# Two graph layers on one core: weight loads, the logit scale, and the first and last pairs of batches rearranged

## The chip, the core and the metric

The kernel runs on one core of one Trainium2 chip. The metric is the device time of one execution in microseconds (us), the median over repeated runs. A profile is one execution recorded by the hardware profiler; its times of single instructions are used below. Five engines work in parallel: PE (matrix products; its weight loads are listed as PEld), DVE (vector), ACT (activation functions, copies with scale and bias), POOL (a second vector engine) and SP (issues transfers). [...]

## The reference, cut to what matters

There are 128 batches of 128 nodes with 512 features, and an adjacency matrix (128 x 128) for each batch. Everything is float32.

```python
# layer 0: 8 heads of 64
q, k, v = (inputs @ W + b for W, b in ((Wq, bq), (Wk, bk), (Wv, bv)))
logits = where(adj > 0, q @ k.T / sqrt(64), -1e9)
out = relu((softmax(logits) @ v) @ Wo + bo)
x = layernorm(x + out)
# layer 1
Wh = x @ W
e = leaky_relu((Wh @ a1)[:, None] + (Wh @ a2)[None, :], 0.2)
h = softmax(where(adj == 0, -1e9, e)) @ Wh
x = layernorm(x + elu(h))
```

## The kernel before

**Pairs and half-size products.** The work is done in 64 pairs of batches (pair p holds batches 2p and 2p+1, called image 0 and image 1 here). The rows of the two images and the halves of the features make a 2 x 2 matrix of blocks on the left, and each weight matrix is cut into 2 x 2 blocks on the right. The product of both is formed with seven block products in place of eight (a scheme of Strassen's kind). That needs sums of left blocks (`left_sums`, L147 to L156: `x_sums`, `o_sums`, `z_sums`, four POOL instructions a pair, on DVE for the last pair), sums of weight blocks (`weight_sums`, L131 to L136, once for each weight: `sums_qk`, `sums_v`, `sums_o`, `sums_w`; the third sum overwrites the block in slot 5 of the tile), and evictions that add partial results. `PRODUCTS` (L139) lists the seven products with their PSUM bank (A, B or C), their left block and their weight slot. Products `qk0` to `qk6` make q and k together with the tile `wqk` (Wq in slots 0 and 1, Wk in slots 5 and 2), `v0` to `v6`, `o0` to `o6` and `w0` to `w6` use `wv_b`, `wo_b` and `w_b`. The evictions are named `p1`, `p1q`, `p1l`, `p6`, `p7`, `c11`, `c12`, `c21`, `c22`. A bank can be written again only when its eviction has read it.

**The stages of a pair.** `load_blocks` and `x_transpose` (DVE) bring x in transposed; `x_sums`; qk products and evictions; `logits` (PE), `mask_logits`, `max_logits` (DVE), `exp_logits`, `norm_logits` (ACT), `weights_t` (DVE) with `weights_out` and `weights_in` (SP: to HBM and back, which finishes the transposition); `mix_values` (PE) and `mix_values_out` (ACT); o products; residual, layer norm (`stats0`, `mean0`, `rstd0`, `shift0`, `norm0`); `edge_term`, `edge_blocks`, `edge_row` (SP), `edge_sums` (ACT), `edge_leaky`, `edge_mask`, `edge_max`, `edge_exp`, `edges_t`, `edges_t_out`, `edges_t_in`; `mix_nodes` (PE) and `mix_nodes_out` (ACT, L630); w products; `elu_exp`, `elu_low`, `elu_max`, `residual1`, the second layer norm and `store`. `mix_values`, `mix_nodes` and the transposed edge weights of the last pair share one PSUM tile named `ps`.

**The two ends.** Pair 0 has no weight sums yet: `qk_plain` (L305) forms its q and k with eight plain products `qk0` to `qk3`, of Wq slot 0, Wq slot 1, Wk slot 5 and Wk slot 2, each for image 0 and image 1. `fold_a`, `fold_t` and `fold_out` (L203 to L225) work out W @ a1 and W @ a2 once: DVE, then four PE transposes each, then ACT. The last pair transposes its softmax weights and its edge weights on PE (L476, L594), and its left sums and two of its elementwise steps run on DVE (`side_engine`, L143).

**What sets the order.** The engines' queues are not filled pair by pair. Each step has a due time: `p * PERIOD + PLAN[step]`, in a planner's unit (78.77 a pair), plus a shift from `ENDS` for pairs near an end; `ENDS` is empty here. All steps of all pairs are sorted by due time (L713) and issued in that order, so each engine's queue is its share of that list. Between pairs 3 and 59 the order repeats; near the ends it is the same list with the missing pairs left out. The weight loads and the scaling of Wq by 1/8 (L198) stand before the list.

Of the kernel before, what the change touches and what calls it, by code (L numbers as in the profile page):

```python
# [17 lines left out]
PERIOD = 78.77  # L18
PLAN = dict(
    load_adj=-214.28, load_blocks=-156.46, x_transpose0=-118.96, x_transpose1=-64.06, qk0=-36.02, x_sums=-35.84,  # L20
    qk1=-32.98, qk_p1=-31.71, fill_logits0=-31.52, sums_v=-30.63, qk4=-28.65, qk_p6=-28.53, qk_p1q=-27.7,
    qk2=-26.32, qk_c11=-24.89, qk3=-22.63, v0=-21.4, qk_p7=-19.94, qk_c22=-19.93, qk5=-14.75, qk6=-13.44,
    qk_c21=-7.89, qk_c12=-7.85, sums_fold1=-6.69, v_p1=-4.73, v1=-4.54, fill_logits1=-1.85, mask=-1.24, v_p6=-0.29,
    logits=0.0, mask_logits0=2.0, max_logits0=3.74, sums_fold_t1=4.13, v3=4.41, v_p7=4.43, v2=7.45, v4=9.21,
    v_c11=9.21, mask_logits1=10.04, load_x1=10.32, v5=13.29, v_c22=14.67, exp_logits0=14.75, v_c21=15.09, v6=17.23,
    v_c12=17.58, max_logits1=22.12, sum_logits0=24.06, norm_logits0=27.41, exp_logits1=33.3, sums_qk=38.84,
    weights_t0=43.7, sum_logits1=43.78, sums_fold_out1=45.25, sums_fold0=46.53, norm_logits1=52.01,
    weights_out0=53.62, weights_t1=55.61, sums_fold_t0=63.24, weights_out1=68.01, weights_in0=70.44,
    sums_fold_out0=71.92, weights_in1=74.3, mix_values0=75.85, sums_w=78.52, mix_values_out0=80.72,
    mix_values1=81.43, mix_values_out1=85.44, load_x0=87.17, sums_o=94.72, o_sums=101.64, o0=106.22, o_p1=113.64,  # L30
    o1=113.67, o4=115.87, o_p6=116.22, o_p1l=117.15, o3=117.16, o_p7=117.32, o2=117.77, o_c11=118.24, o_c22=118.29,
    o5=120.85, o6=121.7, o_c21=121.88, o_c12=122.76, residual01=122.76, stats01=122.82, mean01=123.85,
    residual00=127.73, rstd01=128.28, shift01=128.77, stats00=130.31, norm01=131.24, mean00=131.45, rstd00=133.98,
    edge_term01=134.39, shift00=135.59, edge_term11=137.39, norm00=140.45, edge_term10=144.28, edge_blocks=146.15,
    fill_edges=152.96, edge_row=155.48, edge_term00=159.96, edge_sums=163.39, edge_leaky=169.07, edge_mask=175.0,
    edge_max=179.3, edge_exp=184.85, edges_t=185.93, edges_t_out=188.28, edges_t_in=189.77, mix_nodes1=211.95,
    mix_nodes_out1=218.25, mix_nodes0=220.51, mix_nodes_out0=222.79, z_sums=231.06, w0=248.23, edge_norm=250.39,
    w_p1=253.84, w1=254.02, w2=254.75, w_p6=256.75, w3=258.71, w_c11=259.13, w4=262.95, w_p7=264.55, w5=268.2,
    w_c22=268.29, w6=268.5, w_c21=269.01, w_c12=270.9, elu_exp1=288.36, elu_exp0=298.97, elu_low1=307.12,
    elu_max1=314.12, elu_low0=326.19, elu_max0=338.66, residual10=340.21, stats10=349.64, mean10=349.96,  # L40
    residual11=350.83, rstd10=358.93, stats11=386.25, mean11=395.88, shift10=413.33, rstd11=414.6, shift11=416.7,
    finish0=436.56, finish1=440.87, store0=451.59, store1=492.12)

ENDS = {}

BUFS = dict(
    xb=2, adj=5, xT=3, t=2, scr=1, cw=6, sx=1, pr=2, qT=2, kT=2, mask=2, e1a256=1, u2256=1, cv=2, u3256=1, prb=1,
    e1a512=1, e1b512=1, u2512=1, u3512=1, prT=2, oT=2, so=1, x=3, at=1, e1b256=1, co=6, ejr=1, e=1, atb=1, attT=1,
# [4 lines left out]
def tile_two_graph_layers(ctx: ExitStack, tc: tile.TileContext, x, adj, wq, bq, wk, bk, wv, bv, wo, bo, w, a, out,  # L53
# [36 lines left out]
    def load_blocks(p):  # L90

        XB[p] = buf([P, 2, 4, P], F32, "xb", f"xb_{p}")
        for k in range(4):
            nc.sync.dma_start(XB[p][32 * k:32 * k + 32].rearrange("s i v e -> s (i v) e"), bass.AP(
                tensor=x.tensor, offset=x.offset + 2 * p * P * D + k * P, ap=[[D, 32], [32 * D, 8], [1, P]]))

# [19 lines left out]

    def block_weight(name, width):
        return const.tile([P, 7, 2, width], F32, tag=name, name=name)

    def load_block(t, k, queue, src, rows, cols):  # L120
        for c in range(2):
            queue.dma_start(t[:, k, c, :], src[rows * HALF + c * P:rows * HALF + (c + 1) * P, cols])

    def load_block_x(t, k, queue, src, rows, cols):

        for q in range(4):
            queue.dma_start(t[32 * q:32 * q + 32, k, :, :], bass.AP(
                tensor=src.tensor, offset=src.offset + (q * P + 64 * rows) * D + cols.start,
                ap=[[D, 32], [32 * D, 2], [1, cols.stop - cols.start]]))

    def weight_sums(t, eng):  # L131
        b11, b21, b22, t1, t2, t3, t4 = (t[:, k, :, :] for k in range(7))
        eng.tensor_tensor(t1, t3, b11, op=ALU.subtract)
        eng.tensor_tensor(t2, b22, t1, op=ALU.subtract)  # L134
        eng.tensor_tensor(t3, b22, t3, op=ALU.subtract)
        eng.tensor_tensor(t4, b21, t2, op=ALU.subtract)  # L136
# [10 lines left out]
    def left_sums(tag, p, store):  # L147

        s = SUMS[tag, p] = buf([P, 4, 2, P], F32, f"s{tag}", f"s{tag}_{p}")
# [23 lines left out]
    load_block_x(wqk, 0, nc.scalar, wq, 0, everything)  # L173
    load_block_x(wqk, 1, nc.scalar, wq, 1, everything)
    load_block_x(wqk, 5, nc.sync, wk, 0, everything)
    load_block_x(wqk, 2, nc.sync, wk, 1, everything)
    load_adj(0)
    wv_b, wo_b, w_b = (block_weight(n, HALF) for n in ("wv", "wo", "w"))
    for t, src, load in ((wv_b, wv, load_block_x), (wo_b, wo, load_block), (w_b, w, load_block)):
        load(t, 0, nc.sync, src, 0, lo)  # L180
        load(t, 5, nc.sync, src, 0, hi)
        load(t, 1, nc.sync, src, 1, lo)
        load(t, 2, nc.sync, src, 1, hi)
        if t is wv_b:
            load_blocks(1)
            load_adj(1)
# [10 lines left out]
    for k in range(2):  # L197
        nc.vector.tensor_scalar_mul(wqk[:, k, :, :], wqk[:, k, :, :], qscale)  # L198
# [4 lines left out]
    def fold_a(i):  # L203
# [3 lines left out]
        for c in range(NC):  # L207
            for f in range(2):
                scr = buf([P, HALF], F32, "scr", f"wa_scr{i}_{c}_{f}")
                blk = ((0, 5), (1, 2))[c // 2][f]  # L210
                nc.vector.scalar_tensor_tensor(scr, w_b[:, blk, c % 2, :], 1.0, a_bc[:, f * HALF:(f + 1) * HALF],
                                               op0=ALU.mult, op1=ALU.mult, accum_out=wa[:, f, c:c + 1])
# [10 lines left out]
    def fold_out(i):  # L223
        wa_bc[i] = const.tile([P, D], F32, tag=f"wa_bc{i}", name=f"wa_bc{i}")
        nc.scalar.copy(wa_bc[i], ST.pop(("wa", i)).rearrange("p c k -> p (c k)"))  # L225

# [15 lines left out]
    def rows_product(blk, weight, left, j):  # L242
# [4 lines left out]
        for c in range(2):  # L247
            nc.tensor.matmul(out, left_block(left, blk.pair, a_i, c), weight[:, b_i, c, :], start=first and c == 0,  # L248
# [21 lines left out]

    def layer_norm_mean(key):
        nc.vector.bn_aggr(MV[key], ST.pop(("st", key)))  # L272

    def layer_norm_rstd(key):
        nc.gpsimd.tensor_scalar(RSTD[key], MV[key][:, 1:2], EPS, None, op0=ALU.add)  # L275
        nc.gpsimd.tensor_tensor(RSTD[key], RSTD[key], half, op=ALU.pow)  # L276

    def layer_norm_shift(key):
        NMEAN[key] = small.tile([P, 1], F32, tag="nmean", name=f"nmean_{key}")
# [41 lines left out]
    def with_bias(dst, src, bias):  # L321
        for f in range(NC):
            nc.scalar.activation(dst[:, f * P:(f + 1) * P], src[:, f * P:(f + 1) * P], AF.Identity,
                                 bias=bias[:, f:f + 1], scale=1.0)

    def qk_p1(p):
        b = BL["qk", p]
        if p == 0:
            return
        b.e1k, b.e1q = b.tile("e1a"), b.tile("e1b")  # L330
        with_bias(b.e1k, b.bank["A"], bk_sb)

    def qk_p1q(p):
        b = BL["qk", p]
        if p:
            with_bias(b.e1q, b.bank["A"], bqs)

    def qk_p6(p):
        b = BL["qk", p]
        if p == 0:  # L340
            return
        b.u2 = b.tile("u2")
# [9 lines left out]
    def qk_p7(p):  # L352
        b = BL["qk", p]
        if p == 0:
            return
        b.u3 = b.tile("u3")
# [9 lines left out]
    def qk_c21(p):  # L366
# [3 lines left out]
        else:  # L370
            nc.vector.tensor_add(QK["q", 2 * p + 1], b.bank["B"], b.e1q)
# [8 lines left out]
    def half_product(tag, p, j):  # L380

        if (tag, p) not in BL:
            BL[tag, p] = Blocks(tag, p, HALF)
        weight, left = dict(v=(wv_b, "x"), o=(wo_b, "o"), w=(w_b, "z"))[tag]
        rows_product(BL[tag, p], weight, left, j)

    def half_p1(tag, p):
        b = BL[tag, p]
# [8 lines left out]
    def half_p1l(tag, p):  # L397
        b = BL[tag, p]
        nc.vector.tensor_add(b.e1l, b.bank["A"], bo_bc[:, lo])

    def half_p6(tag, p):
        b = BL[tag, p]
# [3 lines left out]
    def half_c11(tag, p):  # L406
        b = BL[tag, p]
        store = dict(v=V, o=X1, w=Y)[tag]
        for i in range(2):
            store[2 * p + i] = buf([P, D], F32, f"c{tag}", f"c{tag}_{2 * p + i}")  # L410
        b.out = store
        if tag == "o":
# [4 lines left out]
    def half_p7(tag, p):  # L417
        b = BL[tag, p]
# [3 lines left out]
    def half_c22(tag, p):  # L422
        b = BL[tag, p]
        nc.vector.tensor_add(b.out[2 * p + 1][:, hi], b.bank["C"], b.u3)

    def half_c21(tag, p):
        b = BL[tag, p]
        nc.vector.tensor_add(b.out[2 * p + 1][:, lo], b.bank["B"], b.e1l)

    def half_c12(tag, p):  # L430
        b = BL[tag, p]
# [203 lines left out]

    def elu_exp(b):
        t = buf([P, D], F32, "t", f"t_{b}")
        ST["t", b] = t
        nc.scalar.activation(t, Y[b], AF.Exp, scale=RI[b // 2][:, b % 2:b % 2 + 1])

    def elu_low(b):
        t = ST["t", b]
# [96 lines left out]
```

## Time and profile before

| | |
|---|---|
| median of 3 runs | 2425.21 us (2424.7 to 2425.36) |
| the profiled execution's own time | 2427.27 us |
| its span, first to last instruction | 2425.5 us |
| granted PE clock, mean | 0.99 of full speed |
| PE busy | 2375.7 us (98%) |
| PE weight loads busy | 2149.5 us (89%) |
| DVE busy | 1846.5 us (76%) |
| ACT busy | 1558.2 us (64%) |
| POOL busy | 1473.9 us (61%) |
| first product starts | 10.0 us |
| last group of products starts | 2412.2 us |

How to read the views: in the table of stretches each line gives a stretch of the span in us, its length, then for PE, PEld, DVE, ACT and POOL the busy time with the number of instructions in brackets, then the granted PE clock, the share of the transfer engines and GB/s. In the view of waits a line is the waiting engine, tile and line, what it waited for, the total in us, how often, and the longest. In the timeline a line is start, duration, engine, line, operation, tiles and count, and in square brackets the idle time before it with what ended it.

### The profile page before, as it was taken

How to read it: one execution, taken by the hardware profiler on the slowest of the kernel's cores; microseconds unless marked ns; L12 is line 12 of the kernel's file. 1: busy time of each engine (PE TensorE's matmuls, PEld its weight loads, DVE VectorE, ACT ScalarE, POOL GpSimd, SP SyncE). 2: the span in 40 equal slices, each digit the busy share in tenths (PEclk: the TensorE clock that was granted, in tenths of full speed). 3: DMA queues.
4: the chain of work that ended last, by engine and by line, in shares of the span. 5: the costliest groups of instructions: out<-in, count | busy, mean ns of one | idle time of the engine just before them, and what ended most of it. 6: DMA issues, size and time to landing. Idle time of an engine off the chain costs nothing. (4 is left out here: it accounts for less than half of the span.)

```text
span 2425.5 us, 51781 instructions
## 1 busy us (share of the span) xinstructions
PE 2375.7 (98%) x17706; PEld 2149.5 (89%) x17706; DVE 1846.5 (76%) x3897; ACT 1558.2 (64%) x5514; POOL 1473.9 (61%) x1992
## 2 busy tenths in 40 slices
PE   6999999999999999999999999999999999999996
PEld 6899899899899899899899899998998998998984
DVE  5777877777777777777777778778777777777775
ACT  3656766666666666667667667666666666666663
POOL 2546666566566665666666666665665666666656
PEclk8999999999999999999999999999999999999997
DMA  6444354444454354453443443543444544544422
GB/s 148 121 106 112 105 123 115 112 122 115 110 126 114 101 133 112 105 134 105 111 127 105 117 119 107 124 118 107 122 116 111 123 115 103 131 113 104 122 70 60
DMA packets 342631, 275.54 MB, mean 114 GB/s; under 512 B 126625, under 2 KB 292257, under 8 KB 342369
## 3 DMA queue, kind: packets, MB, share of 16 engines
q1 hardware_dynamic: 341392, 270.39, 43.5%
q8 instruction: 142, 2.33, 0.4%
q10 hardware_dynamic: 640, 1.05, 0.2%
q0 software_dynamic: 336, 0.79, 0.1%
q14 instruction: 121, 0.98, 0.1%
HBM read 155.85 MB, written 107.87 MB: 109 GB/s over the span
## 5 line engine op out<-in xcount | busy, mean ns | idle before, releaser
L465 ACT ACTIVATE pr<-pr,nmax 128x128 f32<-128x128 f32 x1024 | 395.2, 389 | 0.0
L474 ACT ACTIVATE pr<-pr,tot 128x128 f32<-128x128 f32 x1024 | 314.8, 412 | 50.0 <-DVE tot L469 49.9
L524 ACT ACTIVATE oT<-po,bv 128x128 f32<-128x128 f32 x512 | 144.5, 363 | 294.1 <-PE po L515 294.1
L649 POOL TENSOR_TENSOR cw<-cw,co 128x512 f32<-128x512 f32 x126 | 157.6, 1272 | 235.9 <-DVE cw L646 235.9
L275 POOL TENSOR_SCALAR rstd<-mv 128x1 f32<-128x1 f32 x256 | 101.4, 396 | 294.1 <-DVE mv L272 288.7
L643 POOL TENSOR_SCALAR t<-t 128x512 f32<-128x512 f32 x126 | 276.1, 2192 | 0.1
L259 PE MATMUL pBqk<-sx,wqk 128*128 128x128 f32 x2016 | 247.4, 276 | 3.6 <-DVE wqk L134 3.5
L259 PEld LDWEIGHTS pBqk<-sx,wqk 128*128 128x128 f32 x2016 | 241.6, 193 | 7.1 <-issue 3.9
L259 PE MATMUL pCqk<-sx,wqk 128*128 128x128 f32 x2016 | 246.6, 276 | 0.0
L259 PE MATMUL pAqk<-xT,wqk 128*128 128x128 f32 x2016 | 245.5, 275 | 0.0
L259 PEld LDWEIGHTS pAqk<-xT,wqk 128*128 128x128 f32 x2016 | 235.9, 192 | 7.4
L259 PEld LDWEIGHTS pCqk<-sx,wqk 128*128 128x128 f32 x2016 | 236.3, 193 | 0.0
L450 POOL MEMSET pr<- 128x1024 f32 x128 | 121.8, 952 | 160.9 <-DVE prb L484 160.9
L454 DVE COPY_PREDICATED pr<-mask,s 128x1024 f32<-128x1024 int32 x128 | 172.3, 1346 | 35.7 <-PE s L442 35.7
L465 ACT ACTIVATION_READ_ACCUMULATOR pr<-pr,nmax 128x1 f32 x1024 | 193.0, 189 | 0.0
L546 DVE SCALAR_TENSOR_TENSOR scr<-co,wa_bc 128x512 f32<-128x512 f32 x256 | 173.4, 677 | 4.1 <-ACT co L283 1.9
L276 POOL TENSOR_TENSOR rstd<-rstd,half 128x1 f32<-128x1 f32 x256 | 144.8, 566 | 21.3
L459 DVE TENSOR_REDUCE nmax<-pr 128x8 f32<-128x1024 f32 x128 | 155.7, 1217 | 0.1
L484 DVE STREAM_TRANSPOSE prb<-pr 128x1024 f32<-128x1024 f32 x126 | 155.1, 1231 | 0.0
L625 PE MATMUL pz<-attT,co 128*128 128x128 f32 x1024 | 136.3, 276 | 7.8 <-ACT zT L630 7.8
L515 PE MATMUL po<-prT,cv 128*64 128x128 f32 x2048 | 141.8, 281 | 1.9 <-ACT oT L524 1.2
L248 PE MATMUL pBv<-wv,sx 128*128 128x256 f32 x512 | 139.1, 394 | 2.0 <-DVE wv L134 2.0
(166 smaller groups left out, 5960.2 us busy)
## 6 DMA issues: line engine op xcount, KB each, us to landing
prd<-prb SPq DMA_DIRECT2D x126, 512.0 KB, 3.0
prT<-prd SPq DMA_DIRECT2D x504, 128.0 KB, 3.5
xb<-in_x_dram SPq DMA_DIRECT2D x256, 128.0 KB, 4.0
x<-in_x_dram SPq DMA_DIRECT2D x128, 256.0 KB, 4.3
out_dram<-cw SPq DMA_DIRECT2D x128, 256.0 KB, 3.5
adj<-in_adj_dram SPq DMA_DIRECT2D x64, 128.0 KB, 2.1
ejr<-ej SPq DMA_DIRECT2D x256, 32.0 KB, 3.9
atd<-atb SPq DMA_DIRECT2D x63, 128.0 KB, 1.8
```

Source lines behind the costliest of these rows:

```text
L259: nc.tensor.matmul(out[:, f * P:(f + 1) * P], weight[:, b_i, c, f * P:(f + 1) * P], left_block(left, blk.pair, a_i, c), start=first and f ...
L276: nc.gpsimd.tensor_tensor(RSTD[key], RSTD[key], half, op=ALU.pow)
L454: nc.vector.copy_predicated(PR[b], MASK[p][:, i, :].unsqueeze(1).to_broadcast([P, H, P]), ST.pop(("s", b)).rearrange("p j h k -> p (j h) k"))
L459: nc.vector.tensor_reduce(NMAX[b], PR[b], AX.X, ALU.max, negate=True)
L465: nc.scalar.activation(PR[b][:, h, :], PR[b][:, h, :], AF.Exp, bias=nmax[:, h:h + 1], scale=1.0, accum_out=TOT[b][:, h:h + 1])
L474: nc.scalar.activation(PR[b][:, h, :], PR[b][:, h, :], AF.Copy, scale=tot[:, h:h + 1])
L484: nc.vector.transpose(PRB[b].rearrange("p k h s -> p h k s"), PR.pop(b).rearrange("p h (k r) -> p h k r", r=32))
L515: nc.tensor.matmul(ST["o", b][j * DH:(j + 1) * DH, hp, :], v[:, h * DH:(h + 1) * DH], prT[:, :, j * (H // 2) + hp, :], start=True, stop=True)
L524: nc.scalar.activation(OT[b][:, f, :], po[:, f, :], AF.Identity, bias=bv_sb[:, f:f + 1], scale=1.0)
L546: nc.vector.scalar_tensor_tensor(scr, X1[b], 1.0, wa_bc[s], op0=ALU.mult, op1=ALU.mult, accum_out=acc)
L643: side_engine(b // 2).tensor_scalar(t, t, 1.0, -1.0, op0=ALU.min, op1=ALU.add)
L649: side_engine(b // 2).tensor_tensor(Y[b], Y[b], X1.pop(b), op=ALU.add)
```

## The change

1. **Loads.** Each weight of `wv_b`, `wo_b`, `w_b` gets another layout (both column halves side by side), so that a row half comes in one transfer of 512 KB (Wo, W) or four of 128 KB (Wv): 8, 2 and 2 transfers where there were 16, 8 and 8. x of pair 0 comes image by image, and these and Wq and Wk are issued alternately from SP and ACT, in the order image 0, Wq upper half, image 1, Wq lower half, Wk.
2. **Logit scale.** Wq is no longer scaled by 1/8 on DVE. The evictions of q do it: ACT in `with_bias`, and in `qk_c21` a `scalar_tensor_tensor` in place of `tensor_add`.
3. **Last pair.** Its o and w products are plain. The upper rows of Wo and W, which the sums have overwritten, are read again (`reload`, in place of `o_sums` and `z_sums`). o: bank A holds image 0 and bank B image 1, both 512 wide. w: bank A holds image 1 (512 wide), banks B and C the left and right 256 columns of image 0. The last rows (image 0) go through ELU, sum and statistics by halves, read from PSUM; the right half is done by `tail_exp`, `tail_max` and `tail_sum`, and `tail_norm` normalizes with DVE and stores.
4. **Order.** `PLAN` has four decimals; `sums_qk`, `sums_v` and the folds are due earlier, `sums_o` earlier, `sums_w` later. `ENDS` gives each step of pairs 0, 1, 2 and 60 to 63 a shift of its own. In the pairs between, each engine's order stays as it was but for one swap on DVE: `residual01` now comes ahead of `o_c12`.

The order that this gives on PE: at the start qk0 to qk3 and logits of pair 0, then v0, v1, v4, v3, v2, v6, v5 of pair 0, then qk0, qk4, qk1, qk2, qk3 of pair 1, a fold, v0, a fold, qk5, qk6, v1 of pair 1, mix_values0 of pair 0, logits of pair 1, mix_values1 of pair 0. On DVE there: x_transpose of pair 0, mask, sums_qk, sums_v, mask_logits0, max_logits0, v_p6, mask_logits1, v_p7, v_c22, x_transpose1 of pair 1, sum_logits0, x_transpose0 of pair 1. At the end on PE: mix_values0, w2, w1, w4, w3, mix_values1, w5 (w of pair 61), o0, o2, o1, o3 of pair 63, mix_nodes1 of 62, w6 of 61, mix_nodes0 and w0, w1, w2, w4, w3, w5, w6 of 62, edges_t and mix_nodes1 of 63, w0, mix_nodes0, w2, w1, w3, w4, w6 of 63.

```diff
-PERIOD = 78.77
+PERIOD = 78.768558
 PLAN = dict(
...
-ENDS = {}
+ENDS = {
+    0: dict(
+        qk_p1=-693.3008, qk_p1q=-562.1962, qk_p6=-558.7086, qk0=-497.8592, x_transpose1=-494.0942,
...
     def load_blocks(p):
         XB[p] = buf([P, 2, 4, P], F32, "xb", f"xb_{p}")
+        if p == 0:
+            return
...
+    def load_first(i):
+        for k in range(4):
+            (nc.sync, nc.scalar)[k % 2].dma_start(XB[0][32 * k:32 * k + 32, i], bass.AP(
+                tensor=x.tensor, offset=x.offset + i * P * D + k * P, ap=[[D, 32], [32 * D, 4], [1, P]]))
...
+    SLOT = (0, 2, 3, 4, 5, 1, 6)
     def block_weight(name, width):
-        return const.tile([P, 7, 2, width], F32, tag=name, name=name)
+        return const.tile([P, 7, 2, width] if width == D else [P, 2, 7, width], F32, tag=name, name=name)
+    def right_block(t, k):
+        return t[:, k, :, :] if t.shape[1] == 7 else t[:, :, SLOT[k], :]
+    def load_rows(t, queue, src):
+        for rows in range(2):
+            queue.dma_start(t[:, :, 2 * rows:2 * rows + 2, :].rearrange("p c h e -> p c (h e)"),
+                            src[rows * HALF:(rows + 1) * HALF].rearrange("(c p) e -> p c e", p=P))
...
     def left_sums(tag, p, store):
+        if p == n_pair - 1 and tag != "x":
+            return reload("o" if tag == "o" else "w", tag)
...
-    load_block_x(wqk, 0, nc.scalar, wq, 0, everything)
-    load_block_x(wqk, 1, nc.scalar, wq, 1, everything)
-    load_block_x(wqk, 5, nc.sync, wk, 0, everything)
-    load_block_x(wqk, 2, nc.sync, wk, 1, everything)
+    load_first(0)
+    load_block_x(wqk, 0, wq, 0)
+    load_first(1)
+    load_block_x(wqk, 1, wq, 1)
+    load_block_x(wqk, 5, wk, 0)
+    load_block_x(wqk, 2, wk, 1)
...
-    for k in range(2):
-        nc.vector.tensor_scalar_mul(wqk[:, k, :, :], wqk[:, k, :, :], qscale)
...
-                                 bias=bias[:, f:f + 1], scale=1.0)
+                                 bias=bias[:, f:f + 1], scale=qscale if bias is bqs else 1.0)
...
-            nc.vector.tensor_add(QK["q", 2 * p + 1], b.bank["B"], b.e1q)
+            nc.vector.scalar_tensor_tensor(QK["q", 2 * p + 1], b.bank["B"], qscale, b.e1q, op0=ALU.mult, op1=ALU.add)
...
+    def plain_product(tag, j):
+        bank = PRODUCTS[j][0]
+        if j == 5 or (tag == "o" and bank == "C"):
+            return
+        b = BL[tag, n_pair - 1]
+        weight, rows, store = dict(o=wo_b, w=w_b)[tag], ST["rows", tag], dict(o=OT, w=ZT)[tag]
+        k = int(j in (2, 3, 6))
...
+        cols = everything if tag == "o" or bank == "A" else lo if bank == "B" else hi
+        left = store[n_batch - 2 + (bank == "B" if tag == "o" else bank == "A")]
+        out = b.bank[bank][:, 0:cols.stop - cols.start]
+        for c in range(2):
+            right = weight[:, c, 2:4, :].rearrange("p h e -> p (h e)") if k else rows[:, c, :]
+            nc.tensor.matmul(out, left[:, 2 * k + c, :], right[:, cols], start=first and c == 0,
+                             stop=not first and c == 1)
...
+    def tail_exp(b):
+        ST["t", b] = buf([P, HALF], F32, "u2256", "t_last")
+        nc.scalar.activation(ST["t", b], BL["w", n_pair - 1].bank["C"][:, lo], AF.Exp, scale=row_scale(b))
+    def tail_max(b):
+        t = ST["t", b]
+        nc.vector.tensor_scalar(t, t, 1.0, -1.0, op0=ALU.min, op1=ALU.add)
+        nc.vector.scalar_tensor_tensor(Y[b][:, hi], BL["w", n_pair - 1].bank["C"][:, lo], row_scale(b), t,
+                                       op0=ALU.mult, op1=ALU.max)
+    def tail_sum(b):
+        nc.vector.tensor_tensor(Y[b][:, hi], Y[b][:, hi], X1[b][:, hi], op=ALU.add)
+        layer_norm_stats_of(LAST_ROWS, 1, Y[b][:, hi])
+    def tail_norm(b):
+        mv, rstd = MV[LAST_ROWS], RSTD[LAST_ROWS]
+        nc.vector.bn_aggr(mv, ST.pop(("st", LAST_ROWS)))
+        nc.vector.tensor_scalar(rstd, mv[:, 1:2], EPS, None, op0=ALU.add)
+        nc.gpsimd.tensor_tensor(rstd, rstd, half, op=ALU.pow)
+        nc.vector.tensor_scalar(Y[b], Y[b], mv[:, 0:1], rstd, op0=ALU.subtract, op1=ALU.mult)
         nc.sync.dma_start(out[b], Y.pop(b))
```

## The prediction

> **What bounds the kernel now.** I read the profile from the whole to the ends. The middle first: in the group view of the line that makes `ej`, executed once a pair, I take the first and last start in a stretch of two pairs.
>
> ```profile
> L552 DVE STREAM_TRANSPOSE ej<-ejb x2: 245/245/245, 1226.7 to 1263.4; 128x64 f32<-128x64 f32 x2
> ```
>
> One pair takes 36.7 us. Against 308.3 for the same line, 25 pairs earlier, it is (1226.7 - 308.3) / 25 = 36.74. So 64 pairs cost 64 x 36.74 = 2351.2 us, and the span has 2425.5 - 2351.2 = **74.3 us** beside them. The table of stretches shows where:
>
> ```profile
> 0.00:10.00 10.00, 0.00 (x0) 0.00 (x0) 1.46 (x3) 0.00 (x0) 4.01 (x14) 1.00 0.89 158
> ...
> 20.00:30.00 10.00, 8.17 (x70) 7.71 (x68) 1.93 (x4) 2.66 (x11) 0.00 (x0) 1.00 0.69 179
> 30.00:40.00 10.00, 4.02 (x41) 3.48 (x42) 6.30 (x24) 0.80 (x4) 0.00 (x0) 0.81 0.93 234
> 40.00:50.00 10.00, 7.78 (x37) 6.60 (x36) 8.83 (x13) 5.73 (x25) 3.78 (x5) 0.84 0.06 16
> 50.00:60.00 10.00, 8.64 (x52) 8.50 (x53) 9.69 (x25) 8.60 (x36) 1.47 (x3) 0.66 0.24 80
> ```
> ```profile
> 2340.00:2360.00 20.00, 17.10 (x92) 14.44 (x91) 15.01 (x38) 16.18 (x59) 8.90 (x14) 1.00 0.10 26
> 2360.00:2380.00 20.00, 16.95 (x90) 13.74 (x90) 12.59 (x33) 8.15 (x23) 12.26 (x15) 0.83 0.28 60
> 2380.00:2400.00 20.00, 12.22 (x38) 9.18 (x38) 11.57 (x27) 5.39 (x13) 14.82 (x19) 0.62 0.15 20
> ```
>
> Between 120 and 2340 PE is busy without a gap. So PE bounds the middle, and the ends are where it idles or runs at a lower granted clock (0.81, 0.66, 0.62). The waits of PE name the causes:
>
> ```profile
> PE pAqk L317 <- DVE xT L290: 10.0, 1, 10.0
> PE pz L625 <- ACT zT L630: 7.8, 3, 4.1
> PE pwa L221 <- DVE wa_rep L215: 5.8, 1, 5.8
> PE pAw L248 <- ACT e1aw L395: 4.1, 2, 3.0
> PE pBqk L259 <- DVE wqk L134: 3.5, 1, 3.5
> PE pBv L248 <- DVE wv L134: 2.0, 1, 2.0
> ```
>
> And the timeline of the first products shows the clock itself, and why DVE is late:
>
> ```profile
> 10.00 3.78 PE L317 MATMUL pAqk<-xT,wqk 128*128 128x128 f32 x16 [10.00 <-DVE xT L290]
> ...
> 21.78 1.95 PE L317 MATMUL pDqk<-xT,wqk 128*128 128x128 f32 x16
> ...
> 28.04 0.71 DVE L290 STREAM_TRANSPOSE xT<-xb 128x512 f32<-128x512 f32 x1 [13.09 <-DMA xb<-in_x_dram]
> ```
>
> Sixteen products start 3.4 us apart cold and 1.79 us apart warm. DVE sat 13.09 us before a transposition for pair 1; the sums of Wv, the fold and the masks of pair 0 all stood behind it in its queue.
>
> The 74.3 us are: 10.0 before the first product, 12.1 after the last (2413.4 to 2425.5), and 52.2 inside. Of the last, 27.7 are idle (12.4 up to 120 us, 15.3 from 2340), some 4.5 are work that only ends have (16 more products in pair 0, folds, the transposes of the last pair), and the remaining 20 are slow clock.
>
> **What the skill says.** The Trainium skill, TensorE: Matmul & The Clock Gate, section "What's actually happening": PE runs at half clock until it has been busy about 3.4 us and falls back after an idle window of that length. The trace agrees: 3.4 against 1.79 us, and clock 0.50 at 38 to 42 us, after the idle stretch 34 to 39. So an idle gap is paid twice. DMA: Bandwidth & Descriptors, section "Issuing engines are not separate DMA queues": loads issued by ACT and SP share the same engines, so splitting saves issue time alone. The trace agrees: 136 to 278 GB/s together in the first 9 us. I therefore count bytes, not queues.
>
> **Part 1, loads.** By the per-us stretches 290 KB had arrived by 3 us, 679 by 5, 861 by 6, 1025 by 7. The first product now needs x of both images and the upper half of Wq among what both queues fetch, and the scaling (0.69) stands before the transposes. Afterwards it needs image 0 (256 KB) and that half (512 KB), 768 KB, which had arrived between 5 and 6 us; bo, another 256 KB, shares the time. I take 6.7 for the first product. Bounds: 5.8 (nothing shared) and 9.5 (biases or the other image first). **Gain 3.3** (0.5 to 4.2). The cold products stay: 17.1 us for the eight plain ones (10.0 to 27.1), so q and k are done at 24. Fewer transfers for Wo and W cost nothing; W isn't needed before the fold.
>
> **Part 2, scale.** Two DVE scalings go: 0.69 + 1.43, counted above. ACT with a scale costs what it costs without: L474 does that at 412 ns for 128x128, L323 369; it isn't dearer by more than 0.05, and ACT has 36% idle. `qk_c21`: 692 ns now; a `scalar_tensor_tensor` of 128x512 is 670 to 749 (L531, L646). Nothing measured here has this form with a PSUM operand: between -0.02 and twice 0.69. DVE waits 77.8 us on 63 such evictions, 1.2 each, and 1.09 before the next, so even the upper bound is covered. Zero.
>
> **Part 3 and 4, start.** By my reckoning of the queues with T = 24: logits run to T+2. `sums_qk` takes DVE when Wk has landed (2.8 MB with bo: near 15.5); its third sum waits for the Wk slot 5 products, about 20.4. Behind it stand sums_v and mask_logits0, whose readers are v1 and exp_logits0. The third and fourth of the qk sums (1.2 each) and the four of Wv (0.68 each) end at 25.6, 0.6 after the first logits. v of pair 0 takes 6 us to T+8.4; then qk0 of pair 1 needs x_transpose0, behind sum_logits0: at worst 1.4 late. qk0, qk4, qk1, qk2, qk3 at 1.79 end at T+18. The second fold, 16 x 0.47 on DVE for each, makes its transposes wait some 2; qk5, qk6, v1, mix_values0 and logits end at T+29. POOL's sums_o (4 x 1.27) comes before o_sums and after the fills and is done by T+29, before o0 reads it. SP's queue has the loads of pair 2 and x ahead of weights_out0, all issued by then; none of them waits for a buffer that isn't free. mix_values1 needs the second softmax: exp (3.1) after qk_p1q, norm 2.4, the transposition 1.2, then out and in through HBM (3.0, 1.8 of issuing, 3.5): T+31.6, so 55.6. It started at 70.3 before: 14.7 earlier, the 3.3 included. After that the PE order is nearly the same and PE is full. I take **14** (bounds 9 with two more waits that fall into slow clock, 17 with none of mine).
>
> **End.** The ends are worked from 2340 with the same rows. Before, mix_nodes0 of 61 waited 2.9 behind norm01 and the prT copy on ACT (`ps` is one tile). mix_nodes_out1 now stands ahead of both, but its product waits for norm_logits0 instead: nothing gained. From 2361: mix_values0, w of 61, mix_values1 and o0, o2 (1.72 each, 512 wide) run to 2371; o1 waits for mix_values_out1, which stands on ACT behind edge_sums and edge_exp of 62. Their `ejr` lands 6.85 after edge_row (2361.17 to 2368.02), so o1 starts at 2372.7, o3 ends at 2376.2 (before: o6 at 2380.6). mix_nodes1 of 62 needs the transposed edges: 2379, 1.8 earlier. The 4.1 wait behind it is mostly gone, since norm00 of 63 is long done: w0 of 62 at 2382.5 against 2388.7. w of 62 follows to 2387.5, its last two products later (DVE is blocked by elu_max1 and elu_max0 of 61, behind POOL's 2.2 each). The edge chain of 63 starts with norm01 at 2383.8, ejr at 2392.5, edge_exp 2396.2, mix_nodes1 at 2397.3 (2403.2 before). Products: w0, mix_nodes0, w2, w1, w3, w4, w6 = 1.72 + 0.9 + 1.72 + 4 x 0.86 after 1.6 for mix_nodes_out1: 2406.7 warm. PE will have been half idle for 9 us, so I add 3.5 for the clock: 2410. The plain products cost more PE time, eight of 0.86 for seven, twice, which is contained here; for it the last pair loses its eight sums on DVE (0.42 each) and some eviction steps. The two loads that replace those sums stand on SP (0.4 to issue, 3.5 to land or somewhat more for 512 KB). The first waits only until the o products of 62 have read `so`, long before. The second waits for w6 of 62, about 2394.5 by this count, behind edge_row of 63, and delays only stores; it lands near 2398.5, and w0 of 63 starts at 2398.9. Zero, but without cover: up to 3.5. Then tail_exp 0.5, tail_max 0.8, tail_sum 0.8, aggregate, pow and normalize 1.7, the store 3.4 and hand-overs 0.3: 7.5 (12.1 before). 2417.5: **gain 8** (4 if the clock stays low to the end, 11.5 if it is warm).
>
> **Sum.** 14 + 8 = 22 from 2425.5, so 2403.5 for the span. The profiled execution reports 2427.27, the median is 2425.21, 0.3 under this span. I forecast **2403** for the median. In the middle only `residual01` moves ahead of `o_c12`:
>
> ```profile
> 1510.49 0.43 DVE L432 TENSOR_TENSOR co<-pCo,u2o 128x256 f32<-128x256 f32 x1 [0.99 <-PE pCo L248]
> ```
>
> DVE idled 0.99 there, more than the 0.68 of the residual; its bank C is next written at 1512.08. Zero.
>
> **Rivals.** (B) The drain gives nothing: the edge chain of 63 through HBM is as late as before and cold products eat the rest. For it: two `ejr` trips of 6.85 stay. 2425 - 14 = 2411. (C) More than I see: my start waits don't occur (17) and the last products are warm (11.5): 2397. (D) Slower: the swap in the middle. If `residual01` waits instead of filling the gap, o_c12 is late; qk4 waits once that exceeds 1512.08 - 1510.92 = 1.16 us. From there each us costs the 57 unshifted pairs 57 us. At 1.7 us late: 57 x 0.54 - 22 = +9, 2434. Against it: its inputs are done at 1508.3. (E) No change: the new start stalls once on a late transfer (10 us and the slow clock after it) and the drain gives nothing: 2425.
>
> **Chances.** Forecast 0.55, B 0.20, C 0.17, D 0.05, E 0.03. About 0.2% (4.9 us) is what a measurement tells from no change, so faster has 0.92, same 0.03, slower 0.05. The range takes in B and most of C: start 10 to 17 and end 3 to 11.5 added give 2397 to 2412; with a little beyond C, 2394 to 2412.
>
> **What would show it.** First product near 6.7; no PE wait on wv or wqk sums; mix_values1 of pair 0 near 55.6; spacing of `ej` still 36.74; mix_nodes1 of 63 about 20 us before the end (22.3 before: 2403.2 to 2425.5); last product to end 7.5. A spacing over 36.8, or mix_values1 later than 62, would make the forecast wrong.

## The result, and the profile after

The changed kernel takes **2418.48 us** (median of 18 runs, 2416.61 to 2424.82), the kernel before 2424.99 (18 runs): a ratio of 0.9976 [0.9968, 0.9983]. It is faster by 0.24%, or 6.5 us, and not by the 22 that I forecast. Its profiled execution took 2418.05 us with a span of 2416.3; the span before was 2425.5, so the two traces differ by 9.2.

The middle is as forecast. The group view of the line that makes `ej`, two pairs:

```profile
L829 DVE STREAM_TRANSPOSE ej<-ejb x2: 245/245/245, 1219.3 to 1256.0; 128x64 f32<-128x64 f32 x2
```

36.7 us a pair, as before, and 7.4 us ahead of it. The swap of `residual01` and `o_c12` shows in the timeline of DVE, and costs nothing; the wait is shorter because the residual now stands in it:

```profile
1503.05 0.43 DVE L709 TENSOR_TENSOR co<-pCo,u2o 128x256 f32<-128x256 f32 x1 [0.43 <-PE pCo L463]
```

The table of stretches, with the columns of the one before:

```profile
0.00:10.00 10.00, 2.91 (x14) 2.94 (x14) 1.47 (x3) 0.00 (x0) 6.50 (x17) 1.00 0.87 183
...
20.00:30.00 10.00, 10.00 (x89) 9.21 (x88) 9.44 (x11) 4.35 (x18) 0.00 (x0) 1.00 1.07 298
30.00:40.00 10.00, 9.80 (x77) 9.17 (x75) 9.45 (x29) 9.25 (x41) 4.61 (x7) 1.00 0.79 180
40.00:50.00 10.00, 7.34 (x47) 6.63 (x46) 7.43 (x24) 5.08 (x17) 2.08 (x2) 0.85 0.43 139
50.00:60.00 10.00, 10.00 (x100) 8.82 (x99) 7.05 (x9) 3.20 (x12) 5.42 (x7) 0.98 0.66 133
```
```profile
80.00:100.00 20.00, 18.25 (x139) 15.43 (x138) 15.06 (x32) 11.16 (x47) 6.79 (x10) 1.00 0.50 105
100.00:120.00 20.00, 18.09 (x179) 17.27 (x180) 14.96 (x27) 11.38 (x39) 7.92 (x13) 1.00 0.65 161
120.00:140.00 20.00, 18.09 (x100) 15.30 (x97) 12.06 (x29) 13.22 (x55) 6.82 (x8) 1.00 0.18 24
```

From 20 to 60 PE does what it could not before (313 instructions against 200). But from 80 to 140 it idles nearly 2 us in each 20 (before: 1.0 in all the 60), with its clock at full speed. The longest waits of PE over the whole span:

```profile
PE pAqk L545 <- DMA wqk<-in_L_gnn_Wq_dram: 7.1, 1, 7.1
PE pAw L463 <- ACT cv L682: 4.1, 2, 2.1
PE pCw L463 <- DVE cw L694: 3.5, 1, 3.5
PE pwa L433 <- ACT e1av L654: 2.5, 1, 2.5
PE pz L902 <- DMA attT<-atd: 2.4, 1, 2.4
PE pBw L463 <- DVE u2w L667: 1.9, 1, 1.9
PE po L792 <- DMA prT<-prd: 1.9, 1, 1.9
```

The first product starts at 7.1 (10.0 before); the waits for the weight sums are gone. New are waits of PE for evictions of V (`cv`), for `prT`, and for other evictions of W than before (`cw`, `u2w`).

**Where the time went.** I read the start of each pair's logits in both traces. Their difference is the lead of the changed kernel at that point (at pairs 61 to 63 only roughly, since other products have moved past the logits there):

| logits of pair | 0 | 1 | 2 | 3 | 4 | 5 | 30 | 60 | 61 | 62 | 63 |
|---|---|---|---|---|---|---|---|---|---|---|---|
| before | 31.23 | 68.30 | 97.62 | 129.72 | 166.41 | 203.15 | 1121.55 | 2223.63 | 2260.36 | 2297.10 | 2333.84 |
| after | 24.34 | 54.05 | 82.87 | 115.73 | 156.63 | 195.78 | 1114.14 | 2216.14 | 2254.20 | 2294.08 | 2330.31 |
| lead | 6.9 | 14.3 | 14.8 | 14.0 | 9.8 | 7.4 | 7.4 | 7.5 | 6.2 | 3.0 | 3.5 |

At the last o product of pair 62, which stands at the same place in both, the lead is 2352.72 - 2350.75 = 2.0, and at the end of the span 9.2. So the ledger is: **+14.8 at the start, -7.4 between 88 and 165 us, -5.5 between 2216 and 2351, +7.2 in the drain after that**; 9.1 in all. Both gains came, that of the drain in part. The profiled execution of the kernel before was a long one (2427.27, the median is 2424.99), and took 72.8 us from that o product to the end. In two experiments further down with the same last pair and the same order at the end, `e_loads_scale` and `e_end_undone`, this stretch took 70.0 and 71.5, in the changed kernel 65.5. So 1.3 to 2.8 of the 7.2 belong to that one execution, and 4.5 to 6.0 to the change. What I had not counted are the two losses. The one at the start repeats: from pair 2 to pair 5 the lead falls by 6.7 to 8.2 in all five traces that have this stretch as it is here (this one, `e_edges_end`, `e_start_only`, `e_end_cut`, `e_end_undone`).

The first is the sum of four waits of PE between 88 and 170 us, 1.7 + 1.9 + 1.9 + 2.1 = 7.6. In the trace before the view of the same stretch has 1.0, in two lines:

```profile
PE pBo L248 <- DVE u2o L404: 0.7, 1, 0.7
PE pCv L248 <- DVE cv L424: 0.3, 1, 0.3
```

The timelines of ACT and PE in the changed kernel at the first of the four:

```profile
86.00 1.14 ACT L801 ACTIVATE oT<-po,bv 128x128 f32<-128x128 f32 x4 [1.87 <-PE po L792]
90.35 0.69 ACT L846 ACTIVATE e<-ejr,ei 128x128 f32<-128x128 f32 x2 [3.21 <-DMA ejr<-ej]
90.95 0.35 ACT L682 COPY cv<-pAv 128x256 f32<-128x256 f32 x1
```
```profile
86.85 1.03 PE L463 MATMUL pAv<-wv,xT 128*128 128x256 f32 x4
...
91.35 1.13 PE L463 MATMUL pAo<-wo,oT 128*128 128x256 f32 x4 [1.75 <-ACT cv L682]
```

The product in bank A ended near 87.9. Its eviction (`cv`) ran at 90.95, because `edge_sums` (L846) of pair 0 stood ahead of it in ACT's queue and waited for its transfer, `ejr`; and PE could not write bank A again before. Two of the other three waits follow the same way: `edge_sums` of pairs 1 and 2, at 128.59 and 162.59, idles 2.12 and 4.70 for `ejr` (of pair 1 through DVE, where `edge_leaky` waits for it ahead of the evictions of W). The third is for `prT`. At the end it is `edge_sums` of pair 59 (2259.35, idle 3.90) and of pair 61 (2335.59, 3.76); of the 5.5 lost there the view of waits shows 3.6, among them 2.0 for `cv` and 0.9 for `u3v` behind these two. The Trainium skill, Perfetto Trace Analysis, section "Tensor Engine Instruction (MATMUL, LD_WEIGHTS)", says that ACT, DVE and GpSimd take their instructions strictly first in, first out. The trace agrees: `cv` was ready 3 us earlier and did not pass. Such a wait does not always cost as much: in the kernel before, `edge_sums` of pair 0 idles 2.52 for `ejr` (101.40), and PE does not wait for the `cv` that follows on ACT, only the 1.0 for DVE shown above.

In the middle `edge_sums` does not wait for `ejr`. The timeline of ACT in the changed kernel, at the same step of a middle pair:

```profile
1227.59 0.69 ACT L846 ACTIVATE e<-ejr,ei 128x128 f32<-128x128 f32 x2 [1.99 <-DVE scr L823]
```

`ej` was made at 1219.3, 8.3 us before. From `ej` to a possible `edge_sums` the trip took 83.38 to 90.35 = 7.0 for pair 0, 122.31 to 128.59 = 6.3 for pair 1, 155.91 to 162.59 = 6.7 for pair 2. For most of these pairs the shifts in `ENDS` have shortened the room for it. From `edge_blocks` to `edge_sums` the plan has 163.39 - 146.15 = 17.2 units, 8.0 us at 36.74 / 78.77 = 0.466 us a unit. With the shifts it is 15.2 units (7.1 us) for pair 0, 7.7 (3.6) for pair 1, 10.7 (5.0) for pair 2 and 8.7 (4.1) for pair 61. For pair 0 the plan thus leaves enough; in the trace ACT came to its `edge_sums` sooner, 3.8 us after `ej` (90.35 - 3.21 - 83.38). Pair 59 has no shifts; its `edge_row` was held up on SP, as the last section shows.

### The profile page after: what moved, and what is told of

It is laid out like the page before. It is cut to its first block, busy times and chain, and to the rows that moved or that the text cites. A ratio compares the mean times of both kernels' runs of the same rounds, so it can differ in the third digit from the quotient of the medians.

```text
span 2416.3 us, 51728 instructions
## 1 busy us (share of the span) xinstructions
PE 2374.7 (98%) x17690; PEld 2142.1 (89%) x17690; DVE 1860.1 (77%) x3882; ACT 1557.7 (64%) x5512; POOL 1413.6 (59%) x1990
## 3 DMA queue, kind: packets, MB, share of 16 engines
q8 instruction: 142, 2.33, 0.4%
## 4 chain that ended last, share of the span: by engine, by line
PE 92%; DMA 3%; DVE 2%; ACT 1%; SPq 1%; issue 0%; POOLq 0%; ACTq 0%; DVEq 0%
PE pBqk L474 14%; PE pAqk L474 9%; PE pCqk L474 9%; PE pBo L463 7%; PE pBv L463 7%; PE pBw L463 7%; PE po L792 5%; PE s L719 5%; PE pz L902 5%; PE pCw L463 4%; PE pAo L463 4%; PE pCo L463 4%; PE pAv L463 4%; PE pCv L463 4%; PE pAw L463 4%; DMA ejr<-ej 1%
## 5 line engine op out<-in xcount | busy, mean ns | idle before, releaser
L933 POOL TENSOR_SCALAR t<-t 128x512 f32<-128x512 f32 x126 | 246.4, 1956 | 14.5 <-ACT t L929 14.3
L823 DVE SCALAR_TENSOR_TENSOR scr<-co,wa_bc 128x512 f32<-128x512 f32 x256 | 187.1, 731 | 11.6 <-ACT co L511 6.1
L907 ACT COPY zT<-pz 128x512 f32<-128x512 f32 x128 | 75.9, 593 | 105.5 <-PE pz L902 105.5
```

Of the source, the lines that this page charges most:

```text
L823: nc.vector.scalar_tensor_tensor(scr, X1[b], 1.0, wa_bc[s], op0=ALU.mult, op1=ALU.mult, accum_out=acc)
L933: side_engine(b // 2).tensor_scalar(t, t, 1.0, -1.0, op0=ALU.min, op1=ALU.add)
```

## Experiments

Five rounds each, with the kernel before on the same chip (medians 2425.0 to 2425.1). An interval is some 0.1% to each side, so differences below about 3 us between two experiments are not told apart by the medians alone. All kernels are the changed kernel with the edit shown; `ENDS` is edited by adding a line behind it.

**Round 1: the edges earlier, and the shifts apart.** `e_edges_start` gives the edge steps of pairs 0, 1 and 2 the middle's times or earlier:

```python
ENDS[0].update(..., norm01=-12.5, edge_term11=-12.5, ..., edge_blocks=-12.5, edge_row=-21.5267)
ENDS[1].update(stats01=0.0, ..., edge_term10=0.0, edge_blocks=0.0, edge_row=0.0)
ENDS[2].update(residual01=0.6412, stats01=0.589, ..., edge_blocks=0.0, edge_row=0.0)
```

> The changed kernel, but in pairs 0, 1 and 2 the first layer norm, the edge products, edge_blocks and edge_row go back to where they stand in the unshifted order relative to the q and k evictions of the pair two later (earlier by 2 to 21 units); all else as changed. Theory A (the edge rows leave too late, so edge_sums waits on ACT for its transfer, and the evictions behind it hold PE's banks): three of the four PE waits between 88 and 165 us go (1.75, 1.91 and 2.13 us, perhaps the 1.91 for the softmax transfer stays), pair spacing returns, time 5 to 6 us under the changed kernel, about 2412.5. Rival B (PE is simply ahead of the other engines after the short start, and the lead is lost in any order): the waits move to other releasers, time within 1.5 us of 2418.

Measured: 2419.07, ratio 0.9975 [0.9964, 0.9985]. No gain. The waits of `edge_sums` for `ejr` are gone, but the lead, 16.4 at pair 1, falls to 5.4 at pair 4. The timelines of SP and PE in this run show what came instead:

```profile
108.22 2.22 SPq L783 DMA_DIRECT2D prT<-prd  x4
111.28 2.45 SPq L836 DMA_DIRECT2D ejr<-ej  x4
113.77 3.23 SPq L284 DMA_DIRECT2D xb<-in_x_dram  x4
117.10 2.78 SPq L783 DMA_DIRECT2D prT<-prd  x4
```
```profile
123.31 1.97 PE L792 MATMUL po<-prT,cv 128*64 128x128 f32 x16 [6.03 <-DMA prT<-prd]
```

`edge_row` (four transfers, 2.45 us to issue) now stands ahead of the second `weights_in` of pair 2 on SP. With `load_blocks` of pair 5, which stood there already, it makes `prT` late, and PE waits 6.0 for it. The theory in its first form, that it is enough to start the trip earlier, is wrong: the trip begins with an issue on SP, and that queue was full.

`e_edges_end` does the same to pairs 60, 61 and 62, with `edge_row` right behind `edge_blocks`.

> The changed kernel, but in pairs 60, 61 and 62 the same steps stand earlier (by up to 22 units) and edge_row comes right behind edge_blocks, ahead of the transfers of the softmax weights. Theory A: the wait of 2.02 us for an eviction of v of pair 61 behind edge_sums goes, and others of that kind; of the 5.5 us of lead lost between logits of pair 60 and the last o product of pair 62, 2 to 4 come back: about 2415. Rival B: other engines are late there in any order, 2417 to 2419.

Measured: 2432.89, ratio 1.0032 [1.0020, 1.0044]: 14 slower than the changed kernel. The timeline of PE has the wait for `prT` twice, and a third one, for `pr`, further on:

```profile
2301.00 1.45 PE L792 MATMUL po<-prT,cv 128*64 128x128 f32 x16 [4.29 <-DMA prT<-prd]
...
2345.55 1.62 PE L792 MATMUL po<-prT,cv 128*64 128x128 f32 x16 [2.80 <-DMA prT<-prd]
...
2369.26 2.52 PE L758 MATMUL ppT<-ident,pr 128*128 128x128 f32 x8 [2.80 <-ACT pr L751]
```

At 2289.85 SP has issued `weights_out`; then `edge_row` (2292.32) goes out ahead of `weights_in` (2294.84 to 2299.7, both images). The three waits are 9.9 together.

`e_start_only` keeps the shifts of pairs 0, 1 and 2 alone; `e_no_shifts` has none, with the weight sums and folds at the times of the kernel before.

```python
ENDS = {p: s for p, s in ENDS.items() if p >= 0}     # e_start_only
ENDS = {}                                            # e_no_shifts, and the sums' entries in PLAN as before
```

> The changed kernel with the shifts of pairs 60 to 63 removed (those of 0, 1, 2 stay). It separates the two ends. Theory A: the lead of 7.4 us at pair 5 is kept to logits of pair 63, and the drain goes as before but for the plain products and the halves: 2425.0 - 7.4 = 2417.6, less 0 to 2: 2416 to 2418, so the end's shifts are worth about nothing as they stand. Rival (the end's shifts are what gains, by an earlier last edge chain): 2421 or more.

> The changed kernel with no shifts at all and the weight sums and folds at their due times of before: the loads, the scale in the evictions, the plain last pair and the halves alone. Theory A: the first product starts near 7 us (3 earlier), but DVE waits for x of pair 1 ahead of the sums as before, so PE stops later by what it started earlier; the end gains 0 to 2 by the halves. 2421 to 2424. Rival (the lead comes from the loads): 2417 or less.

Measured: 2425.14, ratio 0.9999 [0.9991, 1.0007], and 2426.44, 1.0007 [0.9999, 1.0015]. Both are at the time of the kernel before, and above what was expected; for `e_start_only` it is what the rival gave. Yet in the traces their last logits are 6.1 and 4.7 us ahead of it, and the lead hardly changes from pair 5 (6.2 and 5.1) to there. So it is lost after 2330, and only the plain products and the halves of the last pair are different there. The timeline of PE in `e_start_only`:

```profile
2402.37 3.78 PE L641 MATMUL pAw_last<-rows_w,zT 128*128 128x512 f32 x4 [2.33 <-DMA rows_w<-in_L_gnn_W_dram]
```

The reload of W is 2.3 late, and the plain product after it runs at the low clock (3.78 for what takes 1.88 warm).

**Round 2: what blocks, moved by itself.** `e_sums_late` leaves the transfer where it is and moves the waiting steps behind what they block:

```python
ENDS[0].update(edge_sums=-0.0873, edge_leaky=1.9935, edge_mask=-3.9259, edge_max=-7.7956)
ENDS[1].update(edge_sums=18.8441, edge_leaky=19.3649, edge_mask=13.5355, edge_max=12.3858, edge_exp=7.8854, edges_t=8.8003)
ENDS[2].update(edge_sums=3.5756)
```

> The changed kernel with the instruction that waits for the ejr transfer moved, in pairs 0, 1 and 2, from ahead of the V evictions on ACT (and edge_leaky, which waits for it, on DVE) to behind them; the transfer itself stays where it is. Theory (the start's lead is lost because edge_sums waits for ejr at the head of ACT's queue and the V evictions stand behind it): PE's waits of 1.75 at 91, 1.91 at 131 and 2.13 at 165 us go, the lead over the kernel before at the logits of pair 5 is 13.2 instead of 7.4, and the time is 2418.5 - 5.8 = 2412.7 (2411.5 to 2414.5). Rival (a wait that goes is replaced by the next one, as when the edges were moved): a lead of 5.5 to 9 at pair 5 and 2416.5 to 2420.

Measured: 2415.59, ratio 0.9965 [0.9953, 0.9978], half of the gain expected, and its interval overlaps that of the changed kernel. The waits for `cv` and `u2w` are gone from its trace, others of 1.9 (`u2o`) and 1.5 (`u3o`) have come, and the one for `prT` (1.8) is still there. The lead at pair 5 is 4.1, less than the theory and the rival gave. That profiled execution was the longest of its five runs (2422.66), so I read no sizes from it. That moving the reader is enough by itself is not shown.

`e_start_cured` moves both: pair 0 as in `e_sums_late`; pairs 1 and 2 as in `e_edges_start`, but with `edge_row` of pair 1 and `load_blocks` of pair 5 behind `weights_in` of pair 2:

```python
ENDS[1].update(edge_row=5.0528)
ENDS[5] = dict(load_blocks=10.6139)
```

> The same for pair 0; for pairs 1 and 2 the edges are made at the middle's times instead of later, with edge_row of pair 1 issued behind the weights_in of pair 2 on SP, and load_blocks of pair 5 behind it too. Theory (two queues at fault: ACT behind the ejr wait, and SP's order, since prT of pair 2 came 6.0 late when edge_row stood ahead of it): all four waits between 88 and 165 us go, the lead at the logits of pair 5 is 14, the time 2418.5 - 6.6 = 2412 (2410.5 to 2413.5). Rival (the lead can't be held, whatever the order): a lead of 5 to 9, 2416.5 to 2420.

Measured: **2412.96**, ratio 0.9948 [0.9936, 0.9961], where 2412 was expected. The lead is 12.5 at pair 1 and still 12.3 at pair 5. SP and ACT in this run:

```profile
110.24 4.13 SPq L783 DMA_DIRECT2D prT<-prd  x8
114.48 2.41 SPq L836 DMA_DIRECT2D ejr<-ej  x4
```
```profile
126.09 0.69 ACT L846 ACTIVATE e<-ejr,ei 128x128 f32<-128x128 f32 x2
```

Both `weights_in` go out first, `edge_row` behind them still lands in time, and `edge_sums` of pairs 1 and 2 waits for nothing. That of pair 0 still idles 2.12 for its `ejr` (at 92.14), but behind `cv`. What each part of this edit earns was not run. All the waits of PE from 88 to 170 us are one line:

```profile
PE pBo L463 <- DVE u2o L667: 1.8, 1, 1.8
```

Part of it is still that transfer: on DVE `tot` stands ahead of `u2o`, and idles 0.53 for the softmax that ACT begins after this `edge_sums`.

`e_end_cut` drops the shifts of pairs 60 and 61 for all steps ahead of about 2274 us:

```python
ENDS.update({p: {k: s for k, s in ENDS[p].items() if PLAN[k] > 125 - 78.77 * (p + 4)} for p in (-4, -3)})
```

> The changed kernel without the shifts of pairs 60 and 61 for all steps ahead of about 2274 us (those of later steps, and of pairs 62 and 63, stay). Theory (the late give-back begins with these shifts: weights_in of pair 60 comes later and edge_row of 59 stands behind it): the waits at 2260 and 2264 (2.5 together) go, the lead of 7.5 holds to the logits of 61, the drain from 2351 on is as quick as in the changed kernel, 2415.5 (2414 to 2416.7). Rival (the later steps were what the early shifts made room for): the lead holds to 61, is lost after it, and the time is 2418 or more.

Measured: 2414.80, ratio 0.9956 [0.9943, 0.9968]. The waits at 2260 and 2264 are gone, and the lead holds up to pair 61 (8.9 at pairs 30, 60 and 61). The next blocked step, `edge_sums` of pair 61, still costs PE 2.0 at 2334.

`e_loads_scale` has only the loads and the scale; the rest is the kernel before, but for the swap in the middle:

```diff
+PLAN.update(sums_qk=38.84, sums_v=-30.63, ...); ENDS = {}
...
-        if p == n_pair - 1 and tag != "v":
+        if False:
...
     def plain(tag, p):
-        return p == n_pair - 1 and tag != "v"
+        return False
...
     def last_rows(b):
-        return b == n_batch - 2
+        return False
...
```

> The loads and the scale of the changed kernel alone, with the order of the kernel before and rows products in the last pair. Theory (the loads gain 4.7 which stay, as the run without shifts showed up to the last pair, and the plain products, without an order of their own, lose them): the last logits are 4.7 earlier than in the kernel before, the drain from there takes as long as before (91.7 us), 2420.3 (2419.5 to 2421.5). Rival (the drain is longer for another reason than the plain products): 2424 or more.

Measured: 2419.43, ratio 0.9979 [0.9969, 0.9989]. It is 7.0 below `e_no_shifts`, which has the plain products and halves in addition. **The loads and the scale alone earn 5.6, nearly what the whole change earns.**

**Round 3: does it add up?** `e_end_undone` is `e_loads_scale` with the shifts of pairs 0, 1 and 2 (and the changed due times of the sums), so the changed kernel without its end part.

> The loads, the scale and the shifts of pairs 0, 1 and 2 of the changed kernel; the last pair with rows products and the end in the order of the kernel before. Theory (plain products cost as much without an order of their own as the end's shifts win back, so that the whole end part of the change is worth nothing): the start's lead of 6 to 7.4 is kept to the last logits, the drain takes what it takes in the kernel before, 2425.1 - 7 = 2418 (2416.5 to 2419.5), no difference from the changed kernel's 2418.5. Rival (the end part gains what its drain gains, 7): 2423 or more.

Measured: 2418.31, ratio 0.9972 [0.9961, 0.9984]; the changed kernel has 2418.48. The end part as a whole is worth nothing that can be measured here.

`e_both` joins `e_start_cured` and `e_end_cut`.

> The cured start and the cut end together. Theory (they are two places with nothing in common): their gains over the changed kernel, 5.5 and 3.7, add: 2418.5 - 9.2 = 2409.3 (2408 to 2411). Rival (part of what the cut end showed was a luckier start in that run, whose first logits were 1.5 ahead): 2411 to 2413.

Measured: **2409.20**, ratio 0.9935 [0.9921, 0.9948], 9.3 below the changed kernel. The two cures add. In its trace the lead is 15.7 from pair 3 to pair 30; between 88 and 170 us PE waits once, 1.6 for `sx`.

`e_end_cured` uses the principle at two more places of the end:

```python
ENDS[-3].update(edge_sums=12.7441, edge_leaky=14.7149, edge_mask=8.8355)
ENDS[-2].update(w_p7=7.3168, w_c11=23.3377, w_c22=30.6767, w_c21=30.0568)
```

> The same with the principle of the start used at two places of the end: edge_sums and edge_leaky of pair 61 behind the V evictions of 63, and the four W evictions of pair 62 ahead of the steps of pair 63 that wait for ejr. Theory (steps that wait for ejr at the head of a queue are also what holds the end): the wait of PE at 2334 (1.4 to 2.0) and most of those at 2382 and 2386 (1.8 and 3.6) go, mix_nodes1 of 63 is 2.5 earlier, 2.0 to 2.5 below the run before it: 2407 (2405.5 to 2408.5). Rival (the ejr trip of 63 itself is the path, and the products behind it wait for it anyway): within 1 of the run before it.

Measured: 2409.33, ratio 0.9931 [0.9919, 0.9944]. By the medians nothing is gained. In the trace the waits of PE for W shrink as expected:

```profile
2376.12 1.13 PE L463 MATMUL pBw<-w,zT 128*128 128x256 f32 x4 [0.52 <-DVE u3w L689]
2378.55 1.10 PE L463 MATMUL pCw<-w,sz 128*128 128x256 f32 x4 [1.30 <-DVE cw L694]
2382.81 0.86 PE L879 MATMUL pat<-ident,at 128*128 128x128 f32 x2 [3.15 <-ACT at L864]
```

They were 1.81 and 3.35 in `e_both`. But PE then waits 3.15 for the exponentials of pair 63, behind whose `ejr` trip the end hangs anyway (landing 4.09 us after the issue, by the chain that ended last), and `mix_nodes1` of 63 is 1.8 earlier (2384.13 against 2385.91). The wait at 2328 did not go either; it moved to 2331.6 with the same 1.64. Whether 1 or 2 us were won stays open: the runs of both kernels lie from 2406 to 2411.

## Why the forecast was wrong, point by point

- **Part 1, loads.** First product at 7.1 (forecast 6.7), q and k done at 24.2 (24). But the part alone gave 5.6 instead of 3.3. "Fewer transfers for Wo and W cost nothing; W isn't needed before the fold" left out that the fold was waiting for W: DVE waited 3.5 for it in the kernel before (1.91, 0.33 and 1.22, from 31 to 37 us) and 1.0 in `e_loads_scale`, and the wait of PE at the fold fell from 5.8 to 3.4. To "count bytes, not queues" was too simple: SP took 9.41 us to issue the sixteen transfers of Wv and 4.40 for the eight, and the last of W, behind them, was out at 33.6 before and at 23.9 then. The rates given for it (136 to 278 GB/s) hold from 2 to 9 us only, and do not show what limits them.
- **Part 2, scale.** Zero was right as far as it shows: the spacing is unchanged. It was not run by itself.
- **Part 3 and 4, start.** `mix_values1` of pair 0 started at 56.0 (forecast 55.6) and the lead there was 14 to 15. This reckoning held; that it came within 0.4 is partly luck, since the lead at pair 1 lies between 12.5 and 17.4 in the ten traces that have the same order up to there. **The step that failed is the sentence behind it, "After that the PE order is nearly the same and PE is full."** I had followed the queues up to 56 us. The edges of pairs 0, 1 and 2 come later, at 83 to 163 us, with shifts of their own, and there half of the gain was given back: 7.4 of 14.8, in the four waits of PE. `e_start_cured` shows that it need not be.
- **End.** The drain from 2351 gained 7.2 against the one trace before and 4.5 to 6.0 against two others with the old end (forecast 8 from 2340). The forecast counted in the times of the kernel before; with the lead of 2.0 at 2351 put back, `mix_nodes1` of 63 came at 2395.6 + 2.0 = 2397.6 (forecast 2397.3), the last product ended at 2410.3 (2410), and the end came 8.0 later (7.5). What failed is that the shifts of pairs 60 to 62 ahead of 2340 were counted at nothing: 5.5 lost, 3.7 of it recovered by `e_end_cut` in the medians. I also wrote of the plain products that their cost "is contained here". The experiments put a size to it: without an order of their own the plain products and halves cost 7.0, of which the late reload is 2.3 to 2.5 in two traces ("Zero, but without cover: up to 3.5"); the end's shifts win 6.7 back (2425.14 to 2418.48). What makes up the other 4.6 stays open: PE waits 7.1 for `e1aw` at the end of the trace of `e_no_shifts` and 3.9 in that of `e_loads_scale`, but 3.8 in that of `e_start_only`.
- **Swap in the middle.** Zero, as forecast; rival D did not happen.
- **Sum.** 14 + 8 = 22 against 14.8 - 7.4 - 5.5 + 7.2 = 9.1 in the spans. By medians it is 6.5; the profiled execution of the kernel before took 2.3 more than its median, that of the changed kernel 0.4 less. With the drains of 70.0 and 71.5 in place of 72.8 the ledger gives 6.4 to 7.8.
- **A reading.** Sixteen cold products start 3.58 and 3.54 us apart in the trace before (10.00 to 13.58, 51.25 to 54.79), where I wrote 3.4; no sum rests on it.
- **Rivals.** B, the drain gives nothing: the stretch after 2351 did gain, but the end part as a whole gave nothing that can be measured (2418.31 without it), so B was right of the end in effect, for another reason; it missed what the start gave back. E had the right kind, a new start that stalls on a late transfer, at too small a chance (0.03), and with one stall of 10 where four of 2 came.

My own text held what was needed. In the end part I had read that `ejr` takes 6.85 us and that `mix_values_out1` stands behind it on ACT. I did not put the same question to pairs 0 to 2, where the shifts leave 3.6 to 7.1 us for that trip.

## What to carry to other kernels

When steps are reordered, take each transfer whose reader stands in a compute engine's queue and compare its measured trip with the time that the new order leaves between issue and reader. Where it is short, the loss isn't that of the reader but of everything behind it in the queue; move the reader back, or the issue forward, and in the second case look at what stands behind the issue in SP's queue. Take the time between them from a trace of the new order where there is one; the plan showed enough for pair 0. A gain at the start reaches the end only if every later stretch is as free of waits as before, so a table of the lead by pair says in a minute where it was lost; since two profiled executions of one order differ by a few us, repeat what the ledger says in a second trace.

## What the runs showed of the hardware that I had not expected

- SP's queue is as much a bottleneck in order as a compute engine: four `ejr` transfers of 32 KB took 2.4 to 3.7 us to issue in the changed kernel's stretches around the waits above, as long as four of `xb` with 128 KB each (1.9 to 3.1). The Trainium skill, DMA: Bandwidth & Descriptors, section "Anatomy of one DMA — SWDGE (gpsimd) path", is on transfers that GpSimd issues; it says that waits are done by the sequencer that issues, before dispatch, and not by the transfer engines. The trace agrees for SP, in the changed kernel: `ej` of pair 59 was ready at 2249.94, but `edge_row` went out at 2253.16, behind a `weights_in` that had to wait for its `weights_out` (issued 2247.22, 3.6 us before).
- The same start gave leads at pair 3 of 12.3 (`e_start_cured`) and 15.7 (`e_both`) in two profiled executions. They part before 60 us: the wait of PE at the fold was 4.0 in one and 1.8 in the other. With 12.5 to 17.4 at pair 1 in ten traces, one profile of the start is good to about 2.5 us.
- A wait shorter than 3.4 us can be paid twice. In the prediction I took from the Trainium skill (TensorE: Matmul & The Clock Gate, section "What's actually happening") that PE falls back after an idle window of that length. Here the measurement differs: products ran at about half speed after waits of 2.45 us (the changed kernel at 46.8: 3.53 for sixteen that take 1.95 warm), 2.33 (`e_start_only` at 2402) and 1.94 (`e_sums_late` at 96.5: 1.92 for four that take 1.03), but not after 1.75 and 2.13 (91.4 and 164.6 in the changed kernel). Which of them it hits I could not tell beforehand.
